# Expert blocks of two sizes in a routed decoder layer: 32 blocks of 256 slots and 8 of 128, with the bias loaded ahead of the weights

## The chip, the cores and the metric

One core of one Trainium2 chip runs the kernel. TensorE (PE in the profile; its weight loads are PEld) multiplies, VectorE (DVE) and ScalarE (ACT) work elementwise, GpSimd (POOL) issues indirect transfers, SyncE (SP) issues plain ones, and 16 DMA engines carry them out. The metric is the device time of one execution in microseconds. Lower is better.

## The reference

A decoder layer on x of shape 4 x 1024 x 256, in f32: a scan block, a cross attention on a context of 154 rows, and a causal self-attention block whose feed-forward part is a mixture of eight experts. The change touches the experts alone:

```
h2 = layernorm(a)                                      # 4096 tokens x 256
logits = h2 @ Wr + br                                  # 8 experts
kmask = logits >= top_k(logits, 2)[0][..., -1:]        # the two best
w = softmax(where(kmask, logits, -inf))
mid = gelu(einsum('bsd,edf->bsef', h2, e_w1) + e_b1)   # 256 -> 1024
eo = einsum('bsef,efd->bsed', mid, e_w2) + e_b2        # 1024 -> 256
out = einsum('bse,bsed->bsd', w, eo) + a
```

The kernel computes only the two experts that each token has chosen: 8192 rows of work in all.

## The kernel before, in words

The scan block, the cross attention and the self-attention come first; they take the span up to about 2095 us. While the self-attention runs, each group of 512 tokens is routed. A token's normalized row, its number (column D) and its weight (column D + 1) are scattered by GpSimd into `routed`, a table in device memory with 4096 slots for each expert: expert e owns the slots from 4096 e, filled in order. `slot0` holds the first slot of each expert and `free` the next free one. Unused slots hold a token number that is out of bounds, so that a row taken from there is not written back.

Then comes a table (L1333 to L1366, on VectorE). `cnt` is the number of rows of each expert, then its number of 256-slot blocks; running sums `upto` tell which expert block number n belongs to. `tab` holds two integers for each of NB = 39 blocks: the expert (`who`) and the first slot (`start`). 39 is the most that eight experts can need, since each may end in a block that is only partly filled.

The expert stage is a loop over these blocks (L1401 on). For each block SyncE reads the two numbers from `tab` into registers and issues five loads: `xr` (256 rows of `routed`, 260 KB), `w1` (1 MB, L1406), `w2` (1 MB, L1408), `bias` (4 KB, L1410) and `last` (the second bias, broadcast to 128 partitions, 128 KB, L1412). In the profile both weights carry the name `w`. VectorE copies the token numbers to `to` (L1414) and the weights to `by` (L1416). TensorE transposes the rows (L1421), VectorE scales and shifts them into `hT` (L1422). `expert_block` is the first product: eight chunks of 128 of the 1024 inner columns, each two f32 matmuls (four records in the profile, each with a weight load) into one of three PSUM buffers `ps1` (L1309), followed by ScalarE's gelu with the bias into `mid` (L1310). Here w1 is the stationary operand and the block's slots are the moving columns.

`results` is the second product, called one block later in program order: for each 128 slots j, eight f32 matmuls (sixteen records) of `mid` with `w2` (L1315); then VectorE adds `last` (L1385) and multiplies by the weight (L1386), and GpSimd adds the rows to the output in device memory by an indirect transfer (L1389) with `to` as the index.

All pools of this stage have two buffers, so a load for block n + 2 waits until block n has released its buffer. The instructions of TensorE, VectorE, ScalarE and GpSimd are ordered by the scheduler, which may interleave blocks: in the steady state it puts ten of the second product's matmuls between chunk 3 and chunk 4 of the next block's first product. SyncE's own order is fixed by hand (`manual_schedule`): it is the order of the program, and a load that waits for its buffer holds up all loads behind it.

Of the kernel before, what the change touches and what calls it, by code (L numbers as in the profile page):

```python
# [30 lines left out]
E, FF = 8, 1024  # L31
# [6 lines left out]
NTOK = B * T  # L38
XW = 260
TOPK = 2  # L40
MB = 256
MJ = MB // P

NB = (TOPK * NTOK + E * (MB - 1)) // MB
NOWHERE = float(1 << 24)
BIG = float(1 << 20)
I32 = mybir.dt.int32
# [3 lines left out]
def decoder_layer(ctx: ExitStack, tc: tile.TileContext, out: bass.AP, a: dict):  # L51
    nc = tc.nc
# [10 lines left out]
    def load_x(b):  # L63
# [21 lines left out]
        out=below, in_=below, compare_op=ALU.is_ge, fill=0.0, base=-1, pattern=[[1, P]], channel_multiplier=-1  # L85
# [12 lines left out]
    slot0 = const.tile([P, E], F32, name="slot0")  # L98
# [70 lines left out]
    with ExitStack() as ss:  # L169
        wp = ss.enter_context(tc.tile_pool(name="s_w", bufs=1))  # L170
# [18 lines left out]
        base = a["L0_attn_A_base"].rearrange("(n o) -> n o", o=1)  # L189
# [1113 lines left out]
    def expert_block(w1, w2, bias, hT, n, mp, ps_1):  # L1303

        mid = mp.tile([P, FF // P, n], F32, tag="mid", name="mid")
        for f in range(FF // P):
            ps = ps_1.tile([P, n], F32, tag="ps1", name="ps1")
            for k in range(2):
                nc.tensor.matmul(ps, w1[:, k, f * P : (f + 1) * P], hT[:, k, :], start=k == 0, stop=k == 1)  # L1309
            nc.scalar.activation(mid[:, f, :], ps, AF.Gelu, bias=bias[:, f : f + 1])  # L1310
        return mid
# [5 lines left out]
    with ExitStack() as ss:  # L1317
# [7 lines left out]
        with tc.tile_pool(name="r_ps", bufs=1, space=PSUM) as rps:  # L1325
# [3 lines left out]
        flag = rp.tile([P, 1], I32, name="flag")  # L1329
        nc.vector.tensor_copy(flag, info)  # L1330

        cnt = rp.tile([P, E], F32, name="cnt")
        nc.vector.tensor_sub(cnt, free, slot0)  # L1333
        step_i = rp.tile([P, NTOK // MB], I32, name="step_i")
        nc.gpsimd.iota(step_i, pattern=[[MB, NTOK // MB]], base=0, channel_multiplier=0)
        step = rp.tile([P, 1, NTOK // MB], F32, name="step")
        nc.vector.tensor_copy(step[:, 0, :], step_i)
        begun = rp.tile([P, E, NTOK // MB], F32, name="begun")
        nc.vector.tensor_tensor(
            begun, cnt.unsqueeze(2).to_broadcast([P, E, NTOK // MB]), step.to_broadcast([P, E, NTOK // MB]), ALU.is_gt  # L1340
        )
        nc.vector.tensor_reduce(cnt, begun, AX.X, ALU.add)
        upto = rp.tile([P, E], F32, name="upto")
        nc.vector.tensor_copy(upto, cnt)
        for e in range(1, E):
            nc.vector.tensor_add(upto[:, e : e + 1], upto[:, e - 1 : e], cnt[:, e : e + 1])
        num_i = rp.tile([P, NB], I32, name="num_i")
        nc.gpsimd.iota(num_i, pattern=[[1, NB]], base=0, channel_multiplier=0)
        num = rp.tile([P, NB, 1], F32, name="num")
        nc.vector.tensor_copy(num[:, :, 0], num_i)  # L1350
        past = rp.tile([P, NB, E - 1], F32, name="past")
        nc.vector.tensor_tensor(
            past, num.to_broadcast([P, NB, E - 1]), upto[:, : E - 1].unsqueeze(1).to_broadcast([P, NB, E - 1]), ALU.is_ge
        )
        who = rp.tile([P, NB], F32, name="who")
        nc.vector.tensor_reduce(who, past, AX.X, ALU.add)
        nc.vector.tensor_mul(past, past, cnt[:, : E - 1].unsqueeze(1).to_broadcast([P, NB, E - 1]))
        start = rp.tile([P, NB], F32, name="start")
        nc.vector.tensor_reduce(start, past, AX.X, ALU.add)
        nc.vector.tensor_sub(start, num[:, :, 0], start)  # L1360
        nc.vector.tensor_scalar(start, start, float(MB), None, ALU.mult)
        nc.vector.scalar_tensor_tensor(start, who, float(NTOK), start, ALU.mult, ALU.add)
        nc.vector.tensor_scalar(start, start, float(E * NTOK), None, ALU.min)
        tab = rp.tile([P, 2, NB], I32, name="tab")
        nc.vector.tensor_copy(tab[:, 0, :], who)
        nc.vector.tensor_copy(tab[:, 1, :], start)  # L1366

# [1 line left out]
        with tc.If(many == 0) as branch:  # L1369
            with ExitStack() as sb:  # L1370
                wp = sb.enter_context(tc.tile_pool(name="e_w", bufs=2))
                mp = sb.enter_context(tc.tile_pool(name="e_mid", bufs=2))
                ps_t = sb.enter_context(tc.tile_pool(name="e_pst", bufs=2, space=PSUM))
                ps_1 = sb.enter_context(tc.tile_pool(name="e_ps1", bufs=3, space=PSUM))
                ps_2 = sb.enter_context(tc.tile_pool(name="e_ps2", bufs=2, space=PSUM))

                rows = out.rearrange("b t d -> (b t) d")

                def results(mid, w2, to, last, by):
                    same = {}  # L1380
# [15 lines left out]

                before = None

                sb.enter_context(tc.manual_schedule(engines={mybir.EngineType.SP}))
                for n in range(NB):  # L1400
                    e = nc.sync.value_load(tab[0:1, 0, n : n + 1], min_val=0, max_val=E - 1)  # L1401
                    s0 = nc.sync.value_load(tab[0:1, 1, n : n + 1], min_val=0, max_val=E * NTOK)
                    xr = mp.tile([P, MJ, XW], F32, tag="xr", name="xr")
                    nc.sync.dma_start(out=xr, in_=routed[bass.ds(s0, MB), :].rearrange("(j p) w -> p j w", p=P))
                    w1 = wp.tile([P, 2, FF], F32, tag="w1", name="w1")
                    nc.sync.dma_start(out=w1, in_=a["L0_ffn_e_w1"][bass.ds(e, 1)].rearrange("e (k p) f -> p (e k) f", p=P))  # L1406
                    w2 = wp.tile([P, FF // P, D], F32, tag="w2", name="w2")
                    nc.sync.dma_start(out=w2, in_=a["L0_ffn_e_w2"][bass.ds(e, 1)].rearrange("e (f p) d -> p (e f) d", p=P))  # L1408
                    bias = wp.tile([P, FF // P], F32, tag="bias", name="bias")
                    nc.sync.dma_start(out=bias, in_=b1s[bass.ds(e, 1)].rearrange("e p f -> p (e f)"))  # L1410
                    last = wp.tile([P, D], F32, tag="last", name="last")
                    nc.sync.dma_start(out=last, in_=a["L0_ffn_e_b2"][bass.ds(e, 1)].rearrange("e d -> (e d)").partition_broadcast(P))  # L1412
                    to = mp.tile([P, MJ], I32, tag="to", name="to")
                    nc.vector.tensor_copy(to, xr[:, :, D])  # L1414
                    by = mp.tile([P, MJ], F32, tag="by", name="by")
                    nc.vector.tensor_copy(by, xr[:, :, D + 1])  # L1416
                    hT = mp.tile([P, 2, MB], F32, tag="hT", name="hT")
                    for k in range(2):
                        ps = ps_t.tile([P, MB], F32, tag="tp", name="tp")
                        for j in range(MJ):  # L1420
                            nc.tensor.transpose(ps[:, j * P : (j + 1) * P], xr[:, j, k * P : (k + 1) * P], ident)  # L1421
                        nc.vector.tensor_scalar(hT[:, k, :], ps, g2[:, k : k + 1], b2[:, k : k + 1], ALU.mult, ALU.add)  # L1422
# [66 lines left out]
```

## Time and the profile before

| | us |
|---|---|
| runs of the kernel | 2726.61, 2728.68, 2715.9 (median 2726.61) |
| the profiled execution | 2716.55 |
| its span, first to last instruction | 2714.9 |
| TensorE busy (matmuls) | 2454.8 (90%) |
| VectorE, ScalarE, GpSimd busy | 1337.9, 1014.7, 453.8 |
| last load of the table's result by SyncE, first `xr` | 2096.64 |
| first and last start of the first product (L1309) | 2104.6, 2696.5 |
| mean granted TensorE clock over the span | 0.925 |

A row of the profile names the source line, the engine, the operation, the tiles written and read, the number of instructions, the busy time and the mean of one, then the idle time of that engine just before them and what ended it ("<-ACT mid L1310" is ScalarE's instruction at line 1310 that writes `mid`). In the timeline the first two numbers are the start and the length of a run of like instructions. The end of a matmul is modelled, so paces are better read from starts.

### The profile page before, as it was taken

To read this page: it belongs to the slowest core of one execution; us is meant where nothing else is said; L and a number is where in the kernel's file an instruction comes from. 1 tells how busy PE (TensorE), PEld (TensorE's weight loads), DVE (VectorE), ACT (ScalarE), POOL (GpSimd) and SP (SyncE) were. 2 spreads that over 40 slices of the span, in tenths; PEclk is the share of its full clock that TensorE was granted. 3 is DMA by queue.
4 is the path that set the end of the run, shared out by engine and by line. 5 is a ranking of instruction groups with operands and counts; after the bars stand their busy time and mean duration, and the time that the engine had idled before them with its cause. 6 is when DMAs were issued, how large, how long until landed. Compare 5 with 4: busy or idle time off the path is not lost. (4 is left out here: it accounts for less than half of the span.)

```text
span 2714.9 us, 36189 instructions
## 1 busy us (share of the span) xinstructions
PE 2454.8 (90%) x13582; PEld 1437.0 (53%) x13582; DVE 1337.9 (49%) x2771; ACT 1014.7 (37%) x1554; POOL 453.8 (17%) x641
## 2 busy tenths in 40 slices
PE   5999999996799999999999899999984999999998
PEld 2566665665344444343343333333332888878877
DVE  4758666657344345676566566648643111111111
ACT  2444333432345445535334444353341222222222
POOL 1210000001100000211321231223124121221212
PEclk9999999998789789999798898889896999999999
DMA  4593000000000001000001010100002666665653
GB/s 103 144 278 86 1 1 1 1 0 23 20 14 21 14 21 24 15 6 24 24 17 35 16 45 17 32 20 28 18 22 82 189 170 193 166 183 178 168 177 116
DMA packets 142337, 182.99 MB, mean 67 GB/s; under 512 B 34852, under 2 KB 114956, under 8 KB 142156
## 3 DMA queue, kind: packets, MB, share of 16 engines
q1 hardware_dynamic: 119324, 129.32, 15.6%
q0 software_dynamic: 22832, 51.28, 8.0%
q8 instruction: 110, 1.80, 0.3%
q14 instruction: 71, 0.58, 0.1%
HBM read 107.64 MB, written 61.51 MB: 62 GB/s over the span
## 5 line engine op out<-in xcount | busy, mean ns | idle before, releaser
L821 ACT ACTIVATE pt<-ps_exp 128x1024 f32<-128x1024 f32 (+4 forms) x512 | 438.1, 861 | 553.8 <-PE ps_exp L819 454.1
L819 PE MATMUL ps_exp<-qs,kT 32*128 32x512 f32 (+4 forms) x2048 | 516.9, 600 | 6.2 <-DVE mpad L762 1.9
L755 PE MATMUL ps_max<-kT,qa 32*128 32x512 f32 (+3 forms) x1536 | 368.7, 571 | 12.7 <-ACT pt L821 6.1
L1309 PE MATMUL ps<-hT,w 128*128 128x256 f32 x1248 | 290.1, 387 | 36.9 <-ACT mid L1310 33.0
L1310 ACT ACTIVATE mid<-ps,bias 128x256 f32<-128x256 f32 x312 | 139.5, 472 | 448.8 <-DMA bias<-b1s 335.9
L762 DVE TENSOR_REDUCE mpad<-ps_max 128x2 f32<-128x1024 f32 (+3 forms) x256 | 261.3, 1025 | 89.8 <-PE ps_max L755 85.1
L1315 PE MATMUL ps<-w,mid 128*128 128x256 f32 x1248 | 287.9, 379 | 0.0
L1309 PEld LDWEIGHTS ps<-hT,w 128*128 128x128 f32 x1248 | 236.1, 193 | 84.7 <-ACT mid L1310 48.2
L819 PEld LDWEIGHTS ps_exp<-qs,kT 32*128 32x128 f32 (+1 forms) x2048 | 152.0, 186 | 242.9 <-issue 141.9
L793 PE MATMUL ps_o<-pt,vs 128*32 128x512 f32 (+4 forms) x2048 | 252.0, 563 | 1.8 <-ACT oT L801 1.2
L1315 PEld LDWEIGHTS ps<-w,mid 128*128 128x128 f32 x1248 | 234.5, 190 | 29.9
L1389 POOL DMA_INDIRECT out_dram<-y,to x78 | 120.4, 1543 | 495.0 <-DVE y L1386 486.1
L760 DVE TENSOR_TENSOR ps_max<-ps_max,mask_qk 128x256 f32<-128x256 f32 x256 | 109.7, 428 | 171.0 <-PE ps_max L755 111.6
L825 POOL TENSOR_SCALAR_AFFINE_SELECT pt<-pt 128x256 f32<-128x256 f32 x256 | 104.4, 409 | 529.2 <-ACT pt L821 528.5
L744 DVE TENSOR_REDUCE mpad<-ps_max 128x4 f32<-128x616 f32 x128 | 101.6, 799 | 168.7 <-PE ps_exp L819 112.6
L755 PEld LDWEIGHTS ps_max<-kT,qa 32*128 32x128 f32 x1536 | 125.4, 196 | 74.4 <-ACT pt L821 41.9
L1385 DVE TENSOR_TENSOR y<-ps,last 128x256 f32<-128x256 f32 x78 | 33.1, 425 | 267.1 <-PE ps L1315 267.1
L311 PE MATMUL ps_xz<-xnT,w_in 128*128 128x512 f32 x256 | 125.2, 606 | 0.6 <-ACT xnT L303 0.6
L1414 DVE CAST to<-xr 128x2 int32<-128x2 f32 x39 | 6.6, 169 | 241.6 <-DMA out_dram<-y,to 224.2
L793 PEld LDWEIGHTS ps_o<-pt,vs 128*32 128x32 f32 (+1 forms) x2048 | 42.2, 112 | 147.8 <-issue 111.5
L328 PE MATMUL ps_a<-w,w_a 128*128 128x512 f32 x256 | 119.8, 609 | 0.0
L740 PE MATMUL ps_max<-kT,qa 32*128 32x154 f32 x1024 | 110.4, 337 | 5.0 <-DVE mpad L744 3.2
(266 smaller groups left out, 3183.9 us busy)
## 6 DMA issues: line engine op xcount, KB each, us to landing
w<-in_L_ffn_e_w_dram SPq DMA_DIRECT2D x78, 1024.0 KB, 6.9
routed<-zero POOLq DMA_DIRECT2D x16, 2080.0 KB, 53.1
xr<-routed SPq DMA_DIRECT2D x39, 260.0 KB, 5.3
qa<-close SPq DMA_DIRECT2D x256, 32.0 KB, 1.9
last<-in_L_ffn_e_b_dram SPq DMA_DIRECT2D x39, 128.0 KB, 5.6
xs<-in_x_dram SPq DMA_DIRECT2D x4, 1024.0 KB, 8.9
kT<-close SPq DMA_DIRECT2D x128, 32.0 KB, 2.0
plain<-row SPq DMA_DIRECT2D x8, 512.0 KB, 3.7
```

The costliest lines, as they stand in the source:

```text
L311: nc.tensor.matmul(ps, w_in[:, k, c * P : (c + 1) * P], xnT[:, k, :], start=k == 0, stop=k == 1)
L328: nc.tensor.matmul(ps, w_a[:, k, c * P : (c + 1) * P], w[:, k, :], start=k == 0, stop=k == 3)
L740: nc.tensor.matmul(ps[:, i, (j - j0) * n : (j - j0 + 1) * n], qT[r, j * P : (j + 1) * P], kT[r, c, :n], start=True, stop=True,)
L755: nc.tensor.matmul(ps[:, i, : s1 - s0], qT[r, j * P : (j + 1) * P], kT[r, c, s0:s1], start=True, stop=True)
L762: nc.vector.tensor_reduce(to, ps[:, :, : s1 - s0], AX.X, ALU.max, negate=True)
L793: nc.tensor.matmul(o[0][g * HP : (g + 1) * HP, off:], vs[:n, kt, (4 * c + g) * HV : (4 * c + g) * HV + HP], pts[g // 2][:n, g % 2, off:], ...
L819: nc.tensor.matmul(ps[:n, i, off:], kT[r, c, k0 : k0 + n], shifted[0][r, off:], start=True, stop=True)
L821: nc.scalar.activation(pt[:n, :, off:], ps[:n, :, off:], AF.Exp, scale=HD**-0.5)
L1309: nc.tensor.matmul(ps, w1[:, k, f * P : (f + 1) * P], hT[:, k, :], start=k == 0, stop=k == 1)
L1310: nc.scalar.activation(mid[:, f, :], ps, AF.Gelu, bias=bias[:, f : f + 1])
L1315: nc.tensor.matmul(ps, mid[:, f, j * P : (j + 1) * P], w2[:, f, :], start=f == 0, stop=f == FF // P - 1)
L1389: nc.gpsimd.indirect_dma_start(out=rows, out_offset=bass.IndirectOffsetOnAxis(ap=to[:, j : j + 1], axis=0), in_=y[:, j, :], in_offset=None ...
```

## The change

The 39 blocks of 256 slots become NB = 32 blocks of 256 and NH = 8 of 128. Each expert gets as many whole blocks as it has multiples of 256, one more if the rest is over 128, and a half block if the rest is 1 to 128. The eight experts may need up to 36 whole blocks; those past 32 are cut into two halves each and take half-block places from the end of the list, which then are not needed otherwise. The table is worked out anew on VectorE: `full` and `odd` count whole and half blocks of each expert, `firsts` gives the first slot of each block from running sums, and `start` and `who` are made from these for 40 blocks.

In the loop a half block loads 128 rows and does one of the two column groups (`mj` is 1). SyncE's order becomes `xr`, `bias`, `w1`, `last`, `w2`. The tiles `to` and `by` get four buffers instead of two.

```diff
-NB = (TOPK * NTOK + E * (MB - 1)) // MB
+NB = TOPK * NTOK // MB
+NX = 4
+NH = 8
...
+        for t, off in ((full, HB), (odd, 0)):
+            at_ = numbers(f"at{off}", nst, MB)
+            nc.vector.tensor_scalar(at_, at_, float(off), None, ALU.add)
+            nc.vector.tensor_tensor(
+                begun, each(nst, cnt), at_.rearrange("p (o s) -> p o s", o=1).to_broadcast([P, E, nst]), ALU.is_gt
+            )
+            nc.vector.tensor_reduce(t, begun, AX.X, ALU.add)
+        nc.vector.tensor_sub(odd, odd, full)
...
+        whole = firsts(full, slot0, "whole", num)
+        nc.vector.tensor_copy(start[:, :NB], whole[:, :NB])
...
+        left = firsts(odd, rest, "left", num[:, :NH])
+        for x in range(NX):
+            for i in range(2):
+                h = NH - 1 - 2 * x - i
+                nc.vector.scalar_tensor_tensor(
+                    start[:, NB + h : NB + h + 1], whole[:, NB + x : NB + x + 1], float(i * HB),
+                    left[:, h : h + 1], ALU.add, ALU.min,
+                )
...
-                    for j in range(MJ):
+                    for j in range(mid.shape[2] // P):
...
-                for n in range(NB):
+                for n in range(NB + NH):
+                    mb = MB if n < NB else HB
+                    mj = mb // P
...
-                    nc.sync.dma_start(out=xr, in_=routed[bass.ds(s0, MB), :].rearrange("(j p) w -> p j w", p=P))
+                    nc.sync.dma_start(out=xr[:, :mj, :], in_=routed[bass.ds(s0, mb), :].rearrange("(j p) w -> p j w", p=P))
+                    bias = wp.tile([P, FF // P], F32, tag="bias", name="bias")
+                    nc.sync.dma_start(out=bias, in_=b1s[bass.ds(e, 1)].rearrange("e p f -> p (e f)"))
                     w1 = wp.tile([P, 2, FF], F32, tag="w1", name="w1")
                     nc.sync.dma_start(out=w1, in_=a["L0_ffn_e_w1"][bass.ds(e, 1)].rearrange("e (k p) f -> p (e k) f", p=P))
+                    last = wp.tile([P, D], F32, tag="last", name="last")
+                    nc.sync.dma_start(out=last, in_=a["L0_ffn_e_b2"][bass.ds(e, 1)].rearrange("e d -> (e d)").partition_broadcast(P))
                     w2 = wp.tile([P, FF // P, D], F32, tag="w2", name="w2")
                     nc.sync.dma_start(out=w2, in_=a["L0_ffn_e_w2"][bass.ds(e, 1)].rearrange("e (f p) d -> p (e f) d", p=P))
-                    bias = ...
-                    last = ...
-                    to = mp.tile([P, MJ], I32, tag="to", name="to")
+                    to = mp.tile([P, MJ], I32, tag="to", name="to", bufs=4)
...
-                    mid = expert_block(w1, w2, bias, hT, MB, mp, ps_1)
+                    mid = expert_block(w1, w2, bias, hT[:, :, :mb], mb, mp, ps_1)
```

More of the change, by code (lines that the diff above doesn't have):

```diff
@@ L1330, in decoder_layer, with each, numbers, sums @@
         nc.vector.tensor_copy(flag, info)
+        HB = MB // 2
+        def each(n, per):
+            return per.rearrange("p (e o) -> p e o", o=1).to_broadcast([P, E, n])
+        def numbers(name, n, step):
+            t_i = rp.tile([P, n], I32, name=name + "_i")
+            nc.gpsimd.iota(t_i, pattern=[[step, n]], base=0, channel_multiplier=0)
+            t = rp.tile([P, n], F32, name=name)
+            nc.vector.tensor_copy(t, t_i)
+            return t
+        def sums(src, name):
+            t = rp.tile([P, E], F32, name=name)
+            nc.vector.tensor_copy(t, src)
+            for e in range(1, E):
+                nc.vector.tensor_add(t[:, e : e + 1], t[:, e - 1 : e], src[:, e : e + 1])
+            return t
@@ L1332, in decoder_layer @@
         cnt = rp.tile([P, E], F32, name="cnt")
         nc.vector.tensor_sub(cnt, free, slot0)
[L1334 to L1338, printed above, removed]
+        nst = NTOK // MB
+        full = rp.tile([P, E], F32, name="full")
@@ new lines, in decoder_layer @@
+        odd = rp.tile([P, E], F32, name="odd")
+        begun = rp.tile([P, E, nst], F32, name="begun")
+        for t, off in ((full, HB), (odd, 0)):
[5 more added lines that the diff above has]
+            nc.vector.tensor_reduce(t, begun, AX.X, ALU.add)
@@ new lines, in decoder_layer, with firsts @@
+        nc.vector.tensor_sub(odd, odd, full)
+        def firsts(src, first, name, num):
+            n = num.shape[1]
+            upto = sums(src, name + "_upto")
+            ge = rp.tile([P, n, E], F32, name=name + "_ge")
+            nc.vector.tensor_tensor(
+                ge, num.rearrange("p (n o) -> p n o", o=1).to_broadcast([P, n, E]),
+                upto.rearrange("p (o e) -> p o e", o=1).to_broadcast([P, n, E]), ALU.is_ge,
+            )
+            way = rp.tile([P, E], F32, name=name + "_way")
+            nc.vector.tensor_scalar(way, src, -float(MB), None, ALU.mult)
+            nc.vector.tensor_sub(way[:, : E - 1], way[:, : E - 1], first[:, : E - 1])
+            nc.vector.tensor_add(way[:, : E - 1], way[:, : E - 1], first[:, 1:])
+            nc.vector.memset(way[:, E - 1 :], float(2 * E * NTOK))
+            nc.vector.tensor_mul(ge, ge, way.rearrange("p (o e) -> p o e", o=1).to_broadcast([P, n, E]))
+            t = rp.tile([P, n], F32, name=name)
+            nc.vector.tensor_reduce(t, ge, AX.X, ALU.add)
+            nc.vector.scalar_tensor_tensor(t, num, float(MB), t, ALU.mult, ALU.add)
+            nc.vector.tensor_add(t, t, first[:, 0:1].to_broadcast([P, n]))
+            nc.vector.tensor_scalar(t, t, float(E * NTOK), None, ALU.min)
+            return t
@@ new lines, in decoder_layer @@
+        start = rp.tile([P, NB + NH], F32, name="start")
+        num = numbers("num", NB + NX, 1)
+        whole = firsts(full, slot0, "whole", num)
+        nc.vector.tensor_copy(start[:, :NB], whole[:, :NB])
+        rest = rp.tile([P, E], F32, name="rest")
+        nc.vector.scalar_tensor_tensor(rest, full, float(MB), slot0, ALU.mult, ALU.add)
+        left = firsts(odd, rest, "left", num[:, :NH])
[5 more added lines that the diff above has]
+                    left[:, h : h + 1], ALU.add, ALU.min,
+                )
@@ L1339, in decoder_layer @@
+        past = rp.tile([P, NB + NH, E - 1], F32, name="past")
         nc.vector.tensor_tensor(
-            begun, cnt.unsqueeze(2).to_broadcast([P, E, NTOK // MB]), step.to_broadcast([P, E, NTOK // MB]), ALU.is_gt
-        )
[L1342 to L1355, printed above, removed]
@@ L1356, in decoder_layer @@
-        nc.vector.tensor_reduce(who, past, AX.X, ALU.add)
[L1357 to L1363, printed above, removed]
@@ L1364, in decoder_layer @@
-        tab = rp.tile([P, 2, NB], I32, name="tab")
+            past, start.rearrange("p (n o) -> p n o", o=1).to_broadcast([P, NB + NH, E - 1]),
+            slot0[:, 1:].rearrange("p (o e) -> p o e", o=1).to_broadcast([P, NB + NH, E - 1]), ALU.is_ge,
+        )
+        who = rp.tile([P, NB + NH], F32, name="who")
+        nc.vector.tensor_reduce(who, past, AX.X, ALU.add)
+        tab = rp.tile([P, 2, NB + NH], I32, name="tab")
         nc.vector.tensor_copy(tab[:, 0, :], who)
@@ L1403, in decoder_layer @@
                     xr = mp.tile([P, MJ, XW], F32, tag="xr", name="xr")
-                    nc.sync.dma_start(out=xr, in_=routed[bass.ds(s0, MB), :].rearrange("(j p) w -> p j w", p=P))
+                    nc.sync.dma_start(out=xr[:, :mj, :], in_=routed[bass.ds(s0, mb), :].rearrange("(j p) w -> p j w", p=P))
+                    bias = wp.tile([P, FF // P], F32, tag="bias", name="bias")
+                    nc.sync.dma_start(out=bias, in_=b1s[bass.ds(e, 1)].rearrange("e p f -> p (e f)"))
                     w1 = wp.tile([P, 2, FF], F32, tag="w1", name="w1")
                     nc.sync.dma_start(out=w1, in_=a["L0_ffn_e_w1"][bass.ds(e, 1)].rearrange("e (k p) f -> p (e k) f", p=P))
+                    last = wp.tile([P, D], F32, tag="last", name="last")
+                    nc.sync.dma_start(out=last, in_=a["L0_ffn_e_b2"][bass.ds(e, 1)].rearrange("e d -> (e d)").partition_broadcast(P))
                     w2 = wp.tile([P, FF // P, D], F32, tag="w2", name="w2")
                     nc.sync.dma_start(out=w2, in_=a["L0_ffn_e_w2"][bass.ds(e, 1)].rearrange("e (f p) d -> p (e f) d", p=P))
[L1409 to L1412, printed above, removed]
-                    to = mp.tile([P, MJ], I32, tag="to", name="to")
-                    nc.vector.tensor_copy(to, xr[:, :, D])
-                    by = mp.tile([P, MJ], F32, tag="by", name="by")
-                    nc.vector.tensor_copy(by, xr[:, :, D + 1])
+                    to = mp.tile([P, MJ], I32, tag="to", name="to", bufs=4)
+                    nc.vector.tensor_copy(to[:, :mj], xr[:, :mj, D])
+                    by = mp.tile([P, MJ], F32, tag="by", name="by", bufs=4)
+                    nc.vector.tensor_copy(by[:, :mj], xr[:, :mj, D + 1])
                     hT = mp.tile([P, 2, MB], F32, tag="hT", name="hT")
@@ L1419, in decoder_layer @@
                         ps = ps_t.tile([P, MB], F32, tag="tp", name="tp")
-                        for j in range(MJ):
+                        for j in range(mj):
                             nc.tensor.transpose(ps[:, j * P : (j + 1) * P], xr[:, j, k * P : (k + 1) * P], ident)
-                        nc.vector.tensor_scalar(hT[:, k, :], ps, g2[:, k : k + 1], b2[:, k : k + 1], ALU.mult, ALU.add)
-                    mid = expert_block(w1, w2, bias, hT, MB, mp, ps_1)
+                        nc.vector.tensor_scalar(
+                            hT[:, k, :mb], ps[:, :mb], g2[:, k : k + 1], b2[:, k : k + 1], ALU.mult, ALU.add
+                        )
+                    mid = expert_block(w1, w2, bias, hT[:, :, :mb], mb, mp, ps_1)
                     if before is not None:
```

## The prediction, made before the changed kernel was run

> **What bounds the kernel now.** I read the page first. The change touches the last quarter of the span, and the rows of that stage are these (line, engine, tiles, count, busy time, mean ns, idle time before and what ended it):
>
> ```profile
> L1309 PE MATMUL ps<-hT,w 128*128 128x256 f32 x1248 | 290.1, 387 | 36.9 <-ACT mid L1310 33.0
> L1310 ACT ACTIVATE mid<-ps,bias 128x256 f32<-128x256 f32 x312 | 139.5, 472 | 448.8 <-DMA bias<-b1s 335.9
> L1414 DVE CAST to<-xr 128x2 int32<-128x2 f32 x39 | 6.6, 169 | 241.6 <-DMA out_dram<-y,to 224.2
> ```
>
> TensorE waits 33.0 us in all for ScalarE, and ScalarE 335.9 us for the bias transfer. DVE waits 224.2 us for scatters. The view by windows shows which engine is full there (busy us and instructions of PE, PEld, DVE, ACT, POOL; clock; DMA share; GB/s):
>
> ```profile
> 2130.00:2300.00 170.00, 161.53 (x758) 138.58 (x757) 29.21 (x90) 39.26 (x88) 35.49 (x23) 1.00 0.63 180
> 2300.00:2500.00 200.00, 187.08 (x878) 160.36 (x878) 33.65 (x103) 46.37 (x104) 38.58 (x25) 1.00 0.63 178
> ```
>
> TensorE is busy 94 to 95% at full granted clock, the DMA engines 63%: the stage is TensorE's, and the rest of its time is the wait. One block in the timeline (start, us, engine; call the first product E, L1309, and the second R, L1315):
>
> ```profile
> 2144.07 0.60 PE L1421 MATMUL tp<-ident,xr 128*128 128x128 f32 x4
> 2144.26 0.37 SPq L1408 DMA_DIRECT2D w<-in_L_ffn_e_w_dram  x1
> 2144.50 1.03 PE L1315 MATMUL ps<-w,mid 128*128 128x256 f32 x4
> 2144.87 0.39 SPq L1410 DMA_DIRECT2D bias<-b1s  x1
> 2145.37 2.75 PE L1309 MATMUL ps<-hT,w 128*128 128x256 f32 x12
> ...
> 2147.79 0.38 SPq L1406 DMA_DIRECT2D w<-in_L_ffn_e_w_dram  x1
> 2147.96 2.32 PE L1315 MATMUL ps<-w,mid 128*128 128x256 f32 x10
> 2150.58 1.20 ACT L1310 ACTIVATE mid<-ps,bias 128x256 f32<-128x256 f32 x3 [9.73 <-DMA bias<-b1s]
> 2151.11 4.58 PE L1309 MATMUL ps<-hT,w 128*128 128x256 f32 x20 [0.83 <-ACT mid L1310]
> 2155.53 4.05 PE L1315 MATMUL ps<-w,mid 128*128 128x256 f32 x18
> 2159.42 0.60 PE L1421 MATMUL tp<-ident,xr 128*128 128x128 f32 x4
> ```
>
> SyncE's w2 load waits until R of two blocks earlier has freed the buffer (2144.26). The bias is issued behind it, only 0.5 us before its E starts. E is eight chunks of four matmuls; it gets three done (x12), ten R matmuls cover part of the delay, then TensorE stops until 2151.11. The period is 15.35 us.
>
> **Part 1: the bias ahead of the weights.** What is a block without the wait? Starts give the pace: in block 1, E runs without a wait, 32 matmuls from 2115.65 to 2122.56 (6.91 us), then 28 R matmuls to 2128.60 (0.2157 us each, so 6.90 for 32); the transposes take 0.43. That is 14.24, and the block shown loses 1.11, 0.28 more than its listed 0.83 (ends are modelled, waking takes time). All 37 waits: 33.0 + 37 x 0.28 = 43.4. Cross-check: 36 periods from 2128.60 to 2685.70 average 15.475, or 1.235 over the floor, 45.7 in 37 blocks, clock dip included.
>
> In the new order the bias goes out right behind xr, some 3.4 us after that release and about 12 us before its first ScalarE use; landing took 5.1 to 8.9 us. Its buffer is freed by ScalarE's last activation two blocks earlier, long done in whole blocks. I take the whole 43.4. The move costs: "last" now stands ahead of w2 and waits for DVE's add of the block whose buffer it takes (0.2 + 0.42 us after R), and w2, the two table reads, xr, bias and w1 queue behind it; w2 leaves about 1 us later, w1 0.5 to 1. In the before, w1 left 3.5 us after the release (2159.61 to 2163.13) and landed 7.7 later, at 11.2; at 12.2 it is still 3 us ahead of its E (14.24 + 1.3). Zero, under that cover. In the built order the ten R matmuls no longer stand inside E but behind it: free while the bias is early, 2.16 us per block uncovered if it is not.
>
> One wait also cost clock:
>
> ```profile
> 2584.35 6.27 PE L1309 MATMUL ps<-hT,w 128*128 128x256 f32 x20 [1.98 <-ACT mid L1310]
> ```
>
> After 1.98 us of waiting these 20 took 6.27 instead of 4.58: 1.7 us, gone with the wait. [...]
>
> **Part 2: 32 whole blocks and 8 halves for 39.** Seven whole blocks go: 7 x 14.24 = 99.7. Eight halves come. R halves exactly: 16 x 0.2157 = 3.45. E keeps 32 matmuls and 32 weight loads and streams 128 columns; the nearest row is an f32 product of that form with a new stationary tile each time:
>
> ```profile
> 637.19 3.54 PEld L495 LDWEIGHTS ps_s<-byt,wt 128*128 128x128 f32 x30
> 637.29 3.62 PE L495 MATMUL ps_s<-byt,wt 128*128 128x128 f32 x30
> ```
>
> (3.62 - 0.275) / 29 = 0.115 us, so 32 x 0.115 = 3.69; two transposes 0.22: TensorE needs 7.36. ScalarE's eight activations of 128 columns lie between 0.35 and 0.47 each, 3.8 at most, beside E. The DMA engines have more to do (kind: packets, MB, share of 16 engines over 2090 to 2715):
>
> ```profile
> q1 hardware_dynamic: 73008, 97.46, 47.8%
> q0 software_dynamic: 11472, 9.07, 11.1%
> ```
>
> Per whole block that is 0.478 x 625 / 39 = 7.7 plus 0.111 x 625 / 39 = 1.8 for scatters. A half loads the same weights and half of xr (2310 of 2440 KB, 7.25) and scatters half (0.89): 8.1, over TensorE's 7.36. Transfers are issued two blocks ahead: in halves, w1 leaves 3.5 to 5 us after the release (the bias now waits for ScalarE, 0.5 us after E), lands at about 11 to 12 and is needed at 2 x 7.36 = 14.7; 3 us of lead, eaten at 0.7 per block over eight blocks. The built order puts R right behind its own E there, which leaves that lead whole. A half costs between 7.4 and 8.1; I take 7.8: 62.4. Deeper buffers of "to" and "by" take the 224.2 us off DVE; nobody waits behind it now (next add 4 us later), zero; in halves it would have.
>
> **Part 3: the table.** DVE's work from cnt to tab grows from 41 instructions to 76:
>
> ```profile
> 2089.42 0.37 DVE L1366 CAST tab<-start 128x39 int32<-128x39 f32 x1
> 2096.64 0.40 SPq L1404 DMA_DIRECT2D xr<-routed  x1
> ```
>
> Before, it ran 2082.80 to 2089.79, 0.17 us each; 35 more end it at 2095.7 to 2097. xr waited until 2096.64 for the last scatter into "routed", so most is covered; two table reads (about 1.4 us) follow, and the bias ahead of w1 is 0.6 more. Between 0 and +4; 1.5, by the reads.
>
> **Sum**, against the profiled execution (2716.55: span 2714.9 and 1.65 around it): 2716.55 - 43.4 - 1.7 - 99.7 + 62.4 + 1.5 = 2635.6, or 80.9 less. That execution is near the low end of the runs (2715.9, 2726.61, 2728.68; mean 2723.7), and the earlier stages that vary are untouched, so I add 8: 2644.
>
> **The rivals** (times with the same 8).
> Halves starved: if a half's transfers run one batch after another, it lasts as long as w1 took from the release, 11.2 us: 8 x 3.4 = 27, 2671. For: DMA need above TensorE's. Against: issue two blocks ahead. Chance 0.12.
> Weight loads bound E in halves: at their 0.190 us mean, unoverlapped, E is 6.1, the half 9.8, +16: 2660. Against: L495's 30 loads in 3.54 us, 0.118 apart. [...] Chance 0.05.
> The wait changes its owner (a ps1 buffer, hT, "last") at the old size: 32 x 1.2 = 38, 2682. Chance 0.05.
> Slower: the bias is still late and its cover is gone. It happens if the bias, held by its buffer's wait on ScalarE, leaves within 5.7 us (its landing) of its first use: then each whole block stands 1.11 + 2.16 = 3.3 us, 32 x 3.3 = 105, 2749. It turns the sign from 81 / 32 = 2.5 us per block. Against: 12 us between issue and use. Chance 0.03.
>
> **How the numbers follow.** Forecast 0.75, rivals 0.25. 0.5% is 13.6 us, about what a measurement of this kernel can tell from no change. All cases but the last are faster by more; 0.01 for something in between: faster 0.96, same 0.01, slower 0.03. Range: low, 2635.6 with halves at 7.4 and no table cost, on the low runs, 2630; high, the starved halves and table's worst, 2674. The wait's new owner, the slower case and a tenth of the forecast stay outside.
>
> **What would show it.** In the profile after: no ACT-ended idle on E's row, a period of 14.2 to 14.3 us in whole blocks, clock 1.00, bias landing before E; halves 7.4 to 8.1 us apart with DMA share near 1; first xr at 2097 to 2099. Wrong if halves stand over 9 us apart, if E waits for w in them, or if an R waits for "last" or w2.

## The result, and the profile after

The changed kernel takes 2629.83 us (median of 2630.04, 2629.62, 2617.11 and 2645.33) against 2721.26 for the kernel before (median of four runs on the same chip). The ratio is 0.968, with a 95% interval from 0.9631 to 0.9729. The profiled executions stand at 2630.04 and 2716.55, or 86.5 us apart. The forecast shift was 80.9. The forecast time was 2644, and the median lies 0.2 us under the low end of the stated range.

The same page rows as before (line, engine, tiles, count, busy time, mean ns, idle time before and what ended it):

```profile
L1313 ACT ACTIVATE mid<-ps,bias 128x256 f32<-128x256 f32 (+1 forms) x320 | 141.6, 453 | 371.8 <-PE ps L1312 368.0
L1318 PE MATMUL ps<-w,mid 128*128 128x256 f32 x1152 | 262.3, 379 | 3.1 <-DMA w<-in_L_ffn_e_w_dram 3.1
L1312 PE MATMUL ps<-hT,w 128*128 128x256 f32 (+1 forms) x1280 | 258.1, 360 | 2.8 <-DMA w<-in_L_ffn_e_w_dram 2.8
L1472 DVE CAST to<-xr 128x2 int32<-128x2 f32 (+1 forms) x40 | 6.7, 166 | 272.9 <-DMA xr<-routed 265.9
```

The 33.0 us that the first product (E, now L1312) waited for ScalarE are gone. ScalarE waits for TensorE (368.0), no longer for the bias. `to` waits for its rows, not for an old scatter. What TensorE still waits for are loads: 2.8 us for weights, once, in the first block; 3.1 us for weights in R (now L1318) and 0.4 us for rows, both in the half blocks.

The view by windows (busy us and instructions of PE, PEld, DVE, ACT, POOL; clock; DMA share; GB/s), for whole blocks twice and then for the halves:

```profile
2130.00:2300.00 170.00, 170.00 (x813) 149.30 (x812) 31.31 (x96) 43.81 (x95) 37.04 (x24) 1.00 0.67 194
2300.00:2500.00 200.00, 200.00 (x955) 175.62 (x955) 36.41 (x112) 52.24 (x113) 43.18 (x28) 1.00 0.67 194
2500.00:2628.00 128.00, 117.75 (x678) 105.25 (x676) 24.20 (x80) 36.14 (x93) 27.76 (x18) 0.99 0.71 224
```

TensorE is busy for all of 370 us at full granted clock. One whole block in the timeline:

```profile
2152.55 0.60 PE L1479 MATMUL tp<-ident,xr 128*128 128x128 f32 x4
2153.20 0.34 SPq L1468 DMA_DIRECT2D last<-in_L_ffn_e_b_dram  x1
2153.85 7.07 PE L1312 MATMUL ps<-hT,w 128*128 128x256 f32 x32
2156.14 0.35 SPq L1464 DMA_DIRECT2D bias<-b1s  x1
2156.68 0.59 SPq L1466 DMA_DIRECT2D w<-in_L_ffn_e_w_dram  x1
2160.76 6.21 PE L1318 MATMUL ps<-w,mid 128*128 128x256 f32 x28
2166.80 0.60 PE L1479 MATMUL tp<-ident,xr 128*128 128x128 f32 x4
```

From transposes to transposes it is 14.25 us, and so it is for every whole block but the first. E is one run of 32 (its length in the row is modelled; from 2153.85 to 2160.76 are 6.91). The bias leaves at 2156.14 for a block whose E starts a period after 2153.85, at 2168.1, and whose first activation comes 1.5 us after that: 13.5 us of lead. Before, it left 0.5 us ahead of its E, so 2 us ahead of that activation.

### The profile page after: what moved, and what is told of

It reads as the page before. It is cut to its first block, busy times and chain, and to the rows that moved or that the text cites. A ratio compares the mean times of both kernels' runs of the same rounds, so it can differ in the third digit from the quotient of the medians.

```text
span 2628.0 us, 36042 instructions
## 1 busy us (share of the span) xinstructions
PE 2399.8 (91%) x13506; PEld 1397.8 (53%) x13506; DVE 1337.0 (51%) x2801; ACT 1017.3 (39%) x1562; POOL 445.6 (17%) x636
## 5 line engine op out<-in xcount | busy, mean ns | idle before, releaser
L758 PE MATMUL ps_max<-kT,qa 32*128 32x512 f32 (+3 forms) x1536 | 368.6, 570 | 13.5 <-ACT pt L824 5.2
L1313 ACT ACTIVATE mid<-ps,bias 128x256 f32<-128x256 f32 (+1 forms) x320 | 141.6, 453 | 371.8 <-PE ps L1312 368.0
L1318 PE MATMUL ps<-w,mid 128*128 128x256 f32 x1152 | 262.3, 379 | 3.1 <-DMA w<-in_L_ffn_e_w_dram 3.1
L1312 PE MATMUL ps<-hT,w 128*128 128x256 f32 (+1 forms) x1280 | 258.1, 360 | 2.8 <-DMA w<-in_L_ffn_e_w_dram 2.8
L1312 PEld LDWEIGHTS ps<-hT,w 128*128 128x128 f32 x1280 | 224.3, 191 | 31.9 <-issue 3.6
L1318 PEld LDWEIGHTS ps<-w,mid 128*128 128x128 f32 x1152 | 215.0, 190 | 31.0 <-DMA w<-in_L_ffn_e_w_dram 3.7
L1444 POOL DMA_INDIRECT out_dram<-y,to x72 | 111.1, 1544 | 420.0 <-DVE y L1441 381.9
L1472 DVE CAST to<-xr 128x2 int32<-128x2 f32 (+1 forms) x40 | 6.7, 166 | 272.9 <-DMA xr<-routed 265.9
L765 DVE TENSOR_REDUCE twice<-ps_max 128x2 f32<-128x1024 f32 (+3 forms) x128 | 105.5, 825 | 4.4
```

The costliest lines, as they stand in the source:

```text
L758: nc.tensor.matmul(ps[:, i, : s1 - s0], qT[r, j * P : (j + 1) * P], kT[r, c, s0:s1], start=True, stop=True)
L765: nc.vector.tensor_reduce(to, ps[:, :, : s1 - s0], AX.X, ALU.max, negate=True)
L1318: nc.tensor.matmul(ps, mid[:, f, j * P : (j + 1) * P], w2[:, f, :], start=f == 0, stop=f == FF // P - 1)
L1444: nc.gpsimd.indirect_dma_start(out=rows, out_offset=bass.IndirectOffsetOnAxis(ap=to[:, j : j + 1], axis=0), in_=y[:, j, :], in_offset=None ...
```

## The experiments

The times of any of these kernels spread by some 30 us from run to run, and they follow the granted clock of the earlier stages: the changed kernel took 2615.66 us in an execution at 0.931 over the span, 2630.04 at 0.925 and 2649.39 at 0.914. So the kernels are compared by their expert stage in one profiled execution each, from the first issue of `xr` to the end of the span. A period runs from one block's transposes to the next block's. The first one is listed apart, since it varies for reasons of its own (the last section).

| kernel | stage, us | its first period | the rest |
|---|---|---|---|
| before | 618.2 | 14.65 | 603.6 |
| e1: bias moved, 39 blocks | 571.3 | 12.49 | 558.8 |
| e2: 32 + 8 blocks, bias late | 579.3 | 14.58 | 564.7 |
| changed kernel | 533.5 | 12.28 | 521.2 |
| e3: two buffers of `to`, `by` | 544.3 | 12.71 | 531.6 |
| e4: `last` behind `w2` | 533.55 | 14.40 | 519.2 |
| e5: three weight buffers | 535.4 | 14.02 | 521.4 |
| e6: halves among the whole blocks | 536.9 | 12.59 | 524.3 |
| e7: e6 and e4 together | 531.3 | 12.36 | 518.9 |
| e8: e7 again | 532.8 | 12.34 | 520.5 |
| e9: changed kernel again | 532.6 | 12.95 | 519.7 |

e8 against e7, and e9 against the changed kernel, tell what the last column is good for: the same kernel comes back within about 1.5 us.

**e1, the bias alone.** The loop and the table of before, and only this:

```diff
+                    bias = wp.tile([P, FF // P], F32, tag="bias", name="bias")
+                    nc.sync.dma_start(out=bias, ...)
                     w1 = ...
                     w2 = ...
-                    bias = wp.tile([P, FF // P], F32, tag="bias", name="bias")
-                    nc.sync.dma_start(out=bias, ...)
                     last = ...
```

> The 39 blocks of 256 slots stay, SyncE's order becomes xr, bias, w1, w2, last; nothing else is edited. Measured by the stage from the first xr load to the end of the span: 618.3 us before, 533.5 after. My theory (the bias wait costs 1.18 us in each of 37 blocks, and one dip of the clock 1.7): 45 us less, stage 573, period 14.25 us per whole block, no wait of TensorE for ScalarE; time 2670 to 2677 beside a profiled 2716.6. The rival that the wait only changes its owner: period stays above 15 us, stage 610 or more. The rival that the buffers of 'to' and 'by' matter in whole blocks (they stay at two here): period above 14.25 although the bias is early.

Measured: 2671.9 us (median of four), ratio 0.9838 [0.9757, 0.9919]; the stage is 46.9 us shorter, of which 2.2 lie in the first period. Every later period is 14.25. The page's row of E:

```profile
L1309 PE MATMUL ps<-hT,w 128*128 128x256 f32 x1248 | 277.5, 381 | 2.7 <-DMA w<-in_L_ffn_e_w_dram 2.7
```

One moved load of 4 KB is worth 44.8 us, and no other wait takes its place. The scheduler's order changed with it, so the 44.8 are for both: E stands in one piece here, as in the changed kernel, while in before and in e2 ten R matmuls stand inside it.

**e2, the blocks alone.** The changed kernel with SyncE's old order:

```diff
-                    bias = ...
                     w1 = ...
-                    last = ...
                     w2 = ...
+                    bias = ...
+                    last = ...
```

> The changed kernel with 32 whole and 8 half blocks, but SyncE's old order xr, w1, w2, bias, last. My theory (the two parts add up): whole blocks lose 1.2 us each again, 32 x 1.2 = 38, and halves up to 0.8 each, so the stage is 572 to 578 us, beside 533.5 after and 618.3 before, and the time 38 to 45 above the changed kernel. The rival that the late bias loses its cover, 3.3 us in each whole block: stage 635 or more, slower than before. The rival that halves hide the bias wait or that the parts overlap: stage under 565.

Measured: 2679.47 us, ratio 0.9829 [0.9731, 0.9927]; the stage is 38.9 us shorter. The rows of E and of ScalarE:

```profile
L1312 PE MATMUL ps<-hT,w 128*128 128x256 f32 (+1 forms) x1280 | 268.8, 364 | 42.7 <-ACT mid L1313 38.8
L1313 ACT ACTIVATE mid<-ps,bias 128x256 f32<-128x256 f32 (+1 forms) x320 | 136.3, 451 | 421.1 <-DMA bias<-b1s 328.6
```

With the bias behind the weights the wait stays: 38.8 us on E, and 328.6 on ScalarE for the bias, as before. The two parts add up: without the first period, 44.8 + 38.9 = 83.7, against 82.4 for both. That they add up so well is in part chance. With seven whole blocks fewer to wait in, the bias alone should be worth less in e2's layout; but there a whole block lost 1.35 us on average, against 1.19 in the kernel before, and the stretch from the first half block on took 1.9 us more than in the changed kernel.

**e3, two buffers of `to` and `by` as before.**

```diff
-                    to = mp.tile([P, MJ], I32, tag="to", name="to", bufs=4)
+                    to = mp.tile([P, MJ], I32, tag="to", name="to")
```

(and the same for `by`)

> The changed kernel with two buffers for 'to' and 'by' instead of four. My theory: nothing in whole blocks (period 14.25 us), and in halves VectorE's copy to 'to' waits for the scatter of two blocks earlier, 0 to 1.5 us a half ahead of hT: stage 534 to 545 us beside 533.5. The rival that the deeper buffers are worth something everywhere: period above 14.4 us, stage above 540 from whole blocks. The rival that they are worth nothing anywhere: 533 to 534.

Measured, one execution: 10.4 us more in the last column, all of it in the halves; whole blocks keep 14.25. The costliest place in the timeline:

```profile
2583.77 0.15 DVE L1472 CAST to<-xr 128x1 int32<-128x1 f32 x1 [7.29 <-DMA out_dram<-y,to]
2583.84 0.14 DVE L1474 COPY by<-xr 128x1 f32<-128x1 f32 x1
2583.90 0.72 DVE L1480 TENSOR_SCALAR hT<-tp,ln_g,ln_b 128x128 f32<-128x128 f32 x2
2584.35 5.36 PEld L1312 LDWEIGHTS ps<-hT,w 128*128 128x128 f32 x32 [4.79 <-DVE hT L1480]
2584.36 5.55 PE L1312 MATMUL ps<-hT,w 128*128 128x128 f32 x32 [4.38 <-DVE hT L1480]
```

VectorE stands at `to` until a scatter of two blocks earlier has landed; the scaling of `hT` is queued behind it, and TensorE waits 4.38 us for `hT`. These 32 matmuls then took 5.55 us instead of 3.73, at a granted clock of 0.50 for part of them. Three more waits for `hT` of 0.9 to 1.3 us follow, 7.9 in all with this one; with the 1.8 lost to the clock that is 9.7. So VectorE's wait, 224.2 us in the kernel before, cost nothing in 14-us blocks and costs nearly ten in 7-us blocks. (14 R matmuls from 2568.07 on also ran partly at 0.50, 4.65 us instead of 3.19; they stood behind waits for `w2` and `xr`, not for `to`.)

**e4, `last` behind `w2`.** The changed kernel with the order `xr`, `bias`, `w1`, `w2`, `last`.

> The changed kernel with SyncE's order xr, bias, w1, w2, last instead of xr, bias, w1, last, w2. My theory: whole blocks the same (14.25 us); w2 leaves 0.6 to 1 us earlier in the halves, so the 3.5 us that TensorE waits for w2 and xr there fall to 1 to 3; at the start of the stage w2 of block 0 again moves beside w1, so the first product starts 0.5 to 1.2 us later after the first xr than the 6.87 us of the changed kernel. Stage 531 to 535. The rival that 'last' ahead of w2 is what makes the first product start earlier has the same start; the rival that VectorE's add holds up SyncE in whole blocks would shorten their period: it cannot go under 14.25.

Measured, one execution: R's waits for its weights are gone; TensorE waits 1.50 us for `xr` and 0.36 for `w1` in the halves, 1.9 in all and not 3.5. The periods after the first half block are 8.95, 8.60, 7.68, 7.89, 7.25 and 7.25 against 10.03, 8.81, 9.20, 7.25, 7.25 and 7.25, or 2.2 us less. But in e9, which is the changed kernel again, they are 9.50, 9.08, 7.80, 7.25, 7.25 and 7.25, only 0.5 us more than here, so a gain by the order is not shown for halves at the end. The whole stage is the same (533.55) because this execution's first period is 2.1 longer. The first product starts 7.94 us after the first `xr`, as expected, but not by the order: in e1, with the same order, it starts after 6.71.

**e5, a third buffer for every load of the weights' pool.**

```diff
-                wp = sb.enter_context(tc.tile_pool(name="e_w", bufs=2))
+                wp = sb.enter_context(tc.tile_pool(name="e_w", bufs=3))
```

> The changed kernel with three buffers instead of two for w1, w2, bias and last. In the changed kernel TensorE lost 3.5 us in the halves to late w2 and xr (halves 10.0, 8.8, 9.2 us apart, then 7.25). Theory 'lead' (the transfers are merely issued too late, because SyncE waits for R of two blocks earlier): with a third buffer the waits in the halves go, the halves lie 7.25 to 7.8 us apart, stage 529 to 531 us. Theory 'rate' (the DMA engines cannot carry 8.1 us of transfers per half in 7.25): more lead only moves the wait towards the end; the last halves, which cost 7.25 in the changed kernel, become longer or the sum of the waits stays above 2 us, stage 532 or more. Whole blocks 14.25 in both.

Measured, one execution: five of the halves' periods are 7.28, R waits for nothing, and nothing is gained (521.4). One period is 11.72. In the timeline:

```profile
2580.46 0.33 SPq L1461 DMA_DIRECT2D xr<-routed  x1
2584.96 1.03 PE L1318 MATMUL ps<-w,mid 128*128 128x256 f32 x4
2587.71 0.15 DVE L1472 CAST to<-xr 128x1 int32<-128x1 f32 x1 [8.72 <-DMA xr<-routed]
2587.85 0.42 DVE L1440 TENSOR_TENSOR y<-ps,last 128x256 f32<-128x256 f32 x1
2588.19 0.40 DVE L1480 TENSOR_SCALAR hT<-tp,ln_g,ln_b 128x128 f32<-128x128 f32 x1
2588.69 2.90 PE L1312 MATMUL ps<-hT,w 128*128 128x128 f32 x12 [2.70 <-issue]
```

and by windows:

```profile
2586.00:2588.00 2.00, 0.00 (x0) 0.00 (x0) 0.29 (x3) 0.00 (x0) 0.00 (x0) 1.00 1.05 399
2588.00:2590.00 2.00, 1.31 (x6) 1.34 (x7) 1.17 (x4) 0.00 (x0) 0.87 (x1) 0.62 0.54 157
2590.00:2592.00 2.00, 2.00 (x10) 1.91 (x10) 0.00 (x0) 1.10 (x3) 0.67 (x1) 0.52 0.87 204
```

TensorE's 2.70 us are listed as "issue", ended by nothing. The lines ahead of it tell why: VectorE stood at `to` for the following block's `xr` (issued 2580.46, in use 7.25 later), with an addition and `hT` of the running block queued behind that copy. `xr` lies in another pool, still with two buffers. One late transfer gave way to another while the DMA engines were full (1.05); that fullness made the `xr` late was not tried by itself.

**e6, the halves spread out.** One half block after every four whole ones:

```diff
-                for n in range(NB + NH):
+                order = [n for i in range(NH) for n in (*range(i * NB // NH, (i + 1) * NB // NH), NB + i)]
+                for n in order:
```

> The changed kernel with the halves spread out: one after every four whole blocks; loads, buffers and SyncE's order within a block as they are. Both theories of the halves' waits expect them to go, since each half follows whole blocks that leave the DMA engines idle a third of the time: a half adds 7.3 to 7.6 us to its neighbours' 14.25 each, no wait of TensorE for w or xr after the first block, stage 529 to 531 us. If a half still costs 8 us or more between whole blocks, the cost is in the half itself (order of instructions, ScalarE, hT) and neither holds: stage 535 or more.

Measured, one execution: 536.9, a miss. At its best a half block now adds 7.29 (the two periods it touches are 10.74 and 10.80, less one of 14.25). But in four of seven places the second of these is up to 0.7 longer, and the block behind often starts late too. TensorE's waits, from the second block on:

```profile
PE ps L1312 <- DMA w<-in_L_ffn_e_w_dram: 3.6, 6, 1.1
PE ps L1312 <- DVE hT L1481: 0.4, 1, 0.4
```

**e7, the same with `w2` ahead of `last`** (the edits of e6 and e4 together).

> As the interleaved kernel, and SyncE's order xr, bias, w1, w2, last. With the halves spread out nothing waits for w2 any more, so the order of w2 and last is worth nothing: stage within 1 us of the interleaved kernel, apart from the start of the stage (first product 6.7 to 8.0 us after the first xr in all runs so far, whatever the order). If w2's place matters by itself: 2 us or more less.

Measured, one execution: 531.3, and no wait of TensorE at all behind the first block, so the expectation that the order is worth nothing here fell: it is worth 5.4 us in the last column, and 3.8 by e8, the same kernel again. The difference lies in SyncE's queue. In e6 `w2` leaves 0.58 us behind `last`, which itself waits for VectorE's addition. In e7 it leaves ahead of that: measured from the start of the four R matmuls behind the transposes, `w2` leaves at -0.24 us instead of +0.80, and the next `w1` at 3.27 instead of 3.76.

**e8 and e9, e7 and the changed kernel timed side by side.**

> The same kernel as in the run before (a half block after every fourth whole one, and w2 asked for ahead of the last routed rows), now timed. If its stage stays as it was, 531 us from the first gather of routed rows to the end of the span against 533.5 for the changed kernel, it is 2 us better than that kernel, and the ratio to the kernel before should be 0.966 or so. A rival: the single look was a lucky one, the waits for w1 come back (3.6 us or more by TensorE's waits), and the stage is 535 to 537.

> The changed kernel again, on the same chip as the interleaved one, as its yardstick: a stage of 533.5 us with 3.5 us of TensorE waiting in the halves, and a ratio to the kernel before of 0.968. If the interleaved kernel's gain of 2 us is real, it shows in the stages; the times of the two, which spread by 10 us from run to run with the granted clock of the earlier stages, should not tell them apart.

("The last routed rows" in e8's expectation is `last`, the second bias.) Measured, six runs each: 2626.58 us, ratio 0.9669 [0.9623, 0.9714], for e8; 2642.18 us, ratio 0.9711 [0.9662, 0.9760], for e9. The intervals overlap. The stages are 532.8 and 532.6. The waits of e8 behind the second block:

```profile
PE ps L1312 <- DMA w<-in_L_ffn_e_w_dram: 1.3, 2, 1.1
PE ps L1312 <- DVE hT L1481: 0.3, 1, 0.3
```

So e7's single execution was a good one, some of the waits came back, and no version was found that is shown to beat the changed kernel. What is left in the stage would not pay much either: the whole blocks run at TensorE's pace, and eight halves at 7.82 (7.62 in e9) against the 7.29 that one adds here leave 4.2 us (2.6).

## Why the prediction was right, step by step

**The bias wait (43.4 + 1.7 for the clock dip).** Right. From the second period on, 37 periods fell from a mean of 15.44 to 14.25, which is 44.1, and 0.6 more went in the last block: 44.7 against 45.1. e1 gives 44.8 by itself. The step that added 0.28 per block to the listed 0.83, because ends are modelled, is confirmed: the 33.0 of the row alone would have missed 12 us, 1.7 of them the clock dip.

**Seven whole blocks (99.7) for eight halves (62.4).** The sum is right: from the first half block's transposes to the last matmul there are 69.65 us; what a last whole block leaves behind its own period is 7.07 (21.32 in e1 less 14.25); the difference, 62.6, is 7.82 for each of eight. But two of the steps to 7.8 were off, and they offset each other, so that it came out so close is luck (in e9 it is 7.62). The first is the transfers' need, put at 8.1 for a half. The windows of the halves show it (the second one holds no wait):

```profile
2580.00:2592.00 12.00, 10.36 (x66) 9.22 (x65) 2.67 (x10) 2.94 (x8) 3.08 (x2) 1.00 1.06 366
2592.00:2604.00 12.00, 12.00 (x89) 11.40 (x88) 2.71 (x10) 5.89 (x16) 1.54 (x1) 1.00 0.97 339
```

There the blocks follow each other at 7.25 us with the DMA share at 0.97, so a half needs 0.97 x 7.25 = 7.0 us of the engines, a little less than TensorE's 7.25. The second is the lead, of which the forecast let 0.7 us per block be eaten over all eight. In fact it went at once, at the turn from one size to the other. In whole blocks `w2` leaves 13.5 us ahead of its first R (2153.78 to 2167.24); in the second half block one left at 2563.58 and R stood for it until 2571.28. Two blocks later the chain of what ended last (start, length, what) runs through a transfer again:

```profile
2572.82 3.02 PE ps L1318 x14
2575.84 1.90 PE ps L1312 x18
2577.75 10.77 DMA w<-in_L_ffn_e_w_dram
2588.56 1.99 PE ps L1318 x8
2590.77 1.73 PE ps L1318 x8
2592.50 3.57 PE ps L1312 x32
2596.07 1.73 PE ps L1318 x8
```

That `w2`, issued at 2577.75, needs 10.77 us to land, beside the next `xr` and `w1` on full engines (1.06). After these two stops the loads had their lead back: the next `w2` left at 2584.36 for an R at 2595.91, and the last three periods are 7.25. In all R waited 1.47 and 1.64 us for `w2`, and the transposes 0.41 for `xr`; eight halves at the 7.29 of e6 and e7 would be 58.3, so 4.3 us were lost. (The period of 8.81 between the stops holds little of it: there R moves up behind its own E, and 22 R matmuls fall into one period instead of 16.) Two of the signs named for "wrong" did show, single halves over 9 us apart and an R that waits for `w2`: the starved rival's mechanism was there, at 4.3 us and not at 27. e3 shows what the four buffers of `to` and `by` are for: with two the halves cost 10 us more. The prediction had said so without a price.

**The floor of a half block.** 7.36 was forecast, 7.25 measured (2597.63 to 2604.88). The term that was a little large is E: its 32 matmuls took 3.58 from start to start of what follows, not 3.69. So the rival by which weight loads bound E fell:

```profile
2592.12 3.76 PEld L1312 LDWEIGHTS ps<-hT,w 128*128 128x128 f32 x32
2592.33 3.73 PE L1312 MATMUL ps<-hT,w 128*128 128x128 f32 x32
2595.91 1.89 PE L1318 MATMUL ps<-w,mid 128*128 128x256 f32 x8
```

A matmul of 128 columns starts every 0.112 us, each behind a weight load that the page lists at 191 ns. With twice the columns the start comes every 0.2157 us, nearly twice as long, so little of the load's 191 ns shows: 32 loads one after another would be 6.1 us, and E took 3.58, so most of it runs beside matmuls here.

**The table (+1.5, between 0 and +4).** Mis-sized: it measured 0. The last row of the table and the first gather:

```profile
2090.27 0.18 DVE L1420 CAST tab<-who 128x40 int32<-128x40 f32 x1
2091.83 0.98 POOL L1124 DMA_INDIRECT routed<-row,place_i  x1 [0.30 <-issue]
2094.48 0.40 SPq L1461 DMA_DIRECT2D xr<-routed  x1
```

The table ended 6.85 us ahead of the first `xr` before, and 4.03 now: 35 more instructions took 2.8 us, 0.08 each and not the 0.17 that was charged, since many don't depend on each other: additions to the one running sum `upto` start 0.2 us apart before (1.13 for six), while neighbours on different tiles start 0.07 apart now. `xr` leaves 2.65 us behind the start of the last scatter into `routed`, about as before (2.72). So the sign "first xr at 2097 to 2099" was wrong; it was 2094.48, 2.2 earlier than before, by the earlier stages, which the change does not touch.

**The sum.** −44.7 for the waits, −37.2 for the blocks and −2.4 for the first period make −84.3, and the stage measured −84.7; the earlier stages gave the other 2.2 of the span's 86.9. By the forecast's own terms (the last column of the table) it is −82.4 against −82.4; to a tenth that is luck, since e9 in place of the changed kernel gives −83.9. What it lacked were the first period and the start.

**The 8 us on top** were the step that failed. They took the profiled execution for a low one by three runs. Over the 23 runs of the kernel before in this study the mean is 2718.7, only 2.1 above it. The ten runs of the changed kernel average 2635.0. The shift of the means is 83.7.

**The other rivals.** The wait changed no owner at the old size: no whole block after the first waits for anything. The slower case, a late bias with its cover gone, was not tried as such; with the bias late (e2) the scheduler put the R matmuls back inside E.

## What to carry to other kernels

When a wait recurs in every turn of a loop, follow the late transfer back to the queue that issues it: here a load of 4 KB, behind two of 1 MB that wait for buffers, inherited their wait and left only 2 us ahead of its use (44.8 us in all by e1), and moving it cost nothing where the ones it passes had lead (no whole block after the first waits for a weight). Price a smaller tile twice, by the engine and by its transfers, which hardly shrink with it (7.25 us of TensorE here instead of 14.25, but 2310 KB of weights and rows instead of 2440), and look at the turn from one size to the other, where the time between a load's issue and its use shrinks with the period (here from 13.5 us to 7.7, and two waits for `w2`). A wait for a buffer that is harmless at one block size can stop the engine at half of it (the one for `to`: nothing in blocks of 14.25 us, 9.7 us in e3's halves).

## What the runs showed of the hardware beside that

The granted clock changes on a grid. In the changed kernel's trace the stretches of lowered clock (0.50) start at 1930.2, 1984.8, 2032.6 and 2066.7 us, which are 16, 14 and 10 times 3.41 us apart; all 40 such starts in this trace lie on one grid of that step to within 0.04 us, and so do all 45 in that of the kernel before. The one from 2066.7 ends at 2104.3, 9.8 us after the first `xr`; until then the clock is 0.50. The first period goes with two things, when the first product starts and when the full clock comes back:

| kernel | first product, us after first `xr` | clock back, us after first `xr` | first period |
|---|---|---|---|
| e7 | 6.8 | 9.6 | 12.36 |
| changed | 6.9 | 9.8 | 12.28 |
| e8 | 6.5 | 10.0 | 12.34 |
| e1 | 6.7 | 10.1 | 12.49 |
| e6 | 7.0 | 10.4 | 12.59 |
| e3 | 7.0 | 10.5 | 12.71 |
| e9 | 7.1 | 11.1 | 12.95 |
| e5 | 7.3 | 13.1 | 14.02 |
| e4 | 7.9 | 13.2 | 14.40 |
| e2 | 7.8 | 13.2 | 14.58 |
| before | 8.0 | 13.5 | 14.65 |

In the changed kernel the clock came back at the end of a step of the grid that TensorE's busy time in the profile fills to 0.86; the step ahead of it is filled to 0.32. Before, the step is filled to 1.00 and the one ahead of it, filled to 0.62, did not bring the clock back. A full step was not enough everywhere: the one from 2073.6 on in the changed kernel, filled to 1.00 by 16 matmuls of 8 columns, was followed by half clock. By the table the first product ran at half clock for 2.8 to 4.0 us in seven of the traces and for 5.3 to 5.8 in the other four. It starts 0.5 us into a step in the changed kernel and 1.3 us into one before; that its place on the grid decides how long it runs at half clock is a reading of these two, not a test.

```profile
2104.64 9.88 PE L1309 MATMUL ps<-hT,w 128*128 128x256 f32 x32 [3.85 <-DMA w<-in_L_ffn_e_w_dram]
2101.35 8.60 PE L1312 MATMUL ps<-hT,w 128*128 128x256 f32 x32 [2.75 <-DMA w<-in_L_ffn_e_w_dram]
```

These are the first products before and after. Of the 2.4 us between the first periods, 1.1 come from the start (7.99 and 6.87 us after `xr`, by the wait for `w1`) and 1.3 from the clock (5.53 and 2.91 us of the product at half clock). No run ties either to the change: e1 and e4 have the same order of loads and differ by 1.9. Why `w1` lands earlier in some executions stays open.

The grid would also explain which waits cost clock, though this was only argued. A wait of 1.98 us in the kernel before and one of 2.70 in e5 were each followed by 3.4 us at half clock; three waits of 2.01 to 2.03 us in e2 were not (the clock is 1.00 in the windows that hold them), nor were the 1.47 and 1.64 in the changed kernel. Cut along the grid, the steps that TensorE filled to 0.09 and 0.49 (e3), 0.27 (e5) and 0.42 (before) were followed by half clock, and those at 0.47 (before), 0.52 and 0.57 (changed) were not: the share of a step sorts the cases better than the length of the gap, but not cleanly.
